# Giving one of three interleaved lanes an earlier rank in a four-layer graph network kernel

## The chip, the cores and the metric

The kernel runs on one core of one Trainium2 chip. The metric is the device time of one execution in microseconds (us); where several executions are given, it is their median.

## What is computed

The input is `x` (16 x 1024 x 128) and a sparse symmetric-pattern `adj` (16 x 1024 x 1024): about 1.6% of the places off the diagonal, and all on it, are not zero. Four graph layers follow, each applied to a normalized, rectified copy of `x` and added to it:

```python
h = relu(layernorm(x)); x = x + L0(h, adj)   # relu(W [h, (h^T adj)^T / degree] + b)
h = relu(layernorm(x)); x = x + L1(h, adj)   # leaky(W (adj/degree) h + b)
h = relu(layernorm(x)); x = x + L2(h, adj)   # two rounds, below
h = relu(layernorm(x)); x = x + L3(h, adj)   # softmax attention over the neighbours, then elu
```

Layer 2 is the costly one. In each of two rounds it scores every edge (n, m) with a small network, weighs the adjacency with it, sends messages and updates the nodes:

```python
scores = sigmoid(relu(a[:, :, None] + b[:, None] + be1) @ We2 + be2)
messages = (adjacency * scores) @ x
x = layernorm(x + (relu([x, messages] @ Wu1 + bu1) @ Wu2 + bu2)) * gamma + beta
```

## The kernel before, in words

Only the edges are scored. The 1024 x 1024 places of a batch are 64 blocks of 128 x 128; a block (t, u) above the diagonal and its mirror make one "bucket" of up to 320 edges (480 on the diagonal). There are 36 buckets, in nine groups of four (`GROUPS`, L371 to L377). For each bucket the kernel builds one-hot tiles, `on` and `om` and their transposes `onT` and `omT`, with which TensorE gathers node features to edges and scatters scores back to blocks. These tiles live in a pool with as many buffers as one batch needs and four more off the diagonal, so those of the next batch take their places as they come free.

The work of a batch is split into three generators, called lanes here:

- `first` (L533): layer 0 on eight rows of blocks (loads at L547 and L551, degree at L552, transposes at L557, products at L239), layer 1 (`layer1`, L261, rows at L268 to L273), the norm of layer 2, and `build` (L637), which makes the one-hot tiles group by group: a product for ranks (L648, L652), then for each bucket `far` (L618), `on` (L622), `onT` (L660), `omT` (L667) and `om` (L674), with products at L631 and L663 between them.
- `main` (L904): the rounds' lane. Round one, a node update (`update`, L277 to L313), round two. A round (`round`, L690) first splits products of the nodes with the weights into two halves (`split`, L682), and then for each of nine groups gathers (L783, L787, and `hid` at L799), scores (L811, row at L824, turned at L836 to L842), scatters (L855, L876), applies the sigmoid and the adjacency (L884, L885) and sends messages (L890). Scatters and messages lag the gathers by a group and more. Its adjacency loads are issued at L761 on SyncE's queue. At a round's end the messages are copied out (L913).
- `last` (L924): the node update after round two, and layer 3 with eight rows (L336 to L358).

Each lane has its own scratch buffers in SBUF and its own bank or banks of PSUM (L398: two for the rounds, one for `first`, one for `last`); the rounds have four more banks for scores, scatters and messages.

Three lanes are in flight together: `main` of batch b, `last` of batch b - 1 and `first` of batch b + 1. `run` (L943) sets up this for each batch, and `weave` (L965) takes steps from the lanes in turn: each generator yields an estimate of what it emitted, and the lane with the smallest share of its total (`MAIN_US`, `LAST_US`, `FIRST_US`) goes next. `main` is always lane 0. The first batch's `first` and the last batch's `last` stand alone.

The order of emission is not quite the order in the program. Each instruction gets a rank from a counter as it is emitted. When the program is put together, each engine takes, by estimated times, the instruction of the lowest rank among those whose inputs and buffers are ready. The order thus found on each engine is fixed in the program; semaphores then make the engines wait for one another on the chip. Where two lanes compete for an engine, the rank decides; where only one is ready, its rank does not matter.

The norm chain that all lanes have is `center` (L193 to L204): a sum (L196), a scaling (L197), a subtraction (L198), a square (L200), a sum (L201), a scaling (L202), all on VectorE, and a power on POOL (L203). In the node update it stands between L305 and L308 to L311.

Of the kernel before, what the change touches and what calls it, by code (L numbers as in the profile page):

```python
# [1 line left out]

# [38 lines left out]
MAIN_US = 248.0  # L41
FIRST_US = 112.0
LAST_US = 95.0


SPLIT = (0, 1, 0, 0, 1, 0, 1, 0)
# [3 lines left out]
def tile_four_gnn_layers(  # L50
# [335 lines left out]
    class Edges:  # L386
# [556 lines left out]
        def run(self):  # L943
# [8 lines left out]
            for b in range(B):  # L952
                s = self.next
                lanes = [(self.main(s, b), MAIN_US)]
                if b:
                    lanes.append((self.last(done, b - 1), LAST_US))
                if b + 1 < B:
# [7 lines left out]
        def weave(self, lanes):  # L965

            out_of = [[0.0, i, gen, us] for i, (gen, us) in enumerate(lanes)]
            while out_of:
                least = min(out_of, key=lambda v: v[:2])
                us = next(least[2], None)  # L970
                if us is None:
                    out_of.remove(least)
                else:
                    least[0] += us / least[3]
# [155 lines left out]
```

## Time and profile before

| what | us |
|---|---|
| median of 3 executions | 6016.66 |
| lowest and highest | 6015.26, 6018.78 |
| the profiled execution, its own time | 6019.67 |
| its span in the profile | 6017.8 |
| TensorE busy (PE) | 5596.7 |
| TensorE weight loads (PEld), beside the products | 4114.2 |
| VectorE busy (DVE) | 4223.4 |
| ScalarE busy (ACT) | 3237.2 |
| one batch in the steady part, from round two to round two | about 361 |

The mean granted clock of TensorE is 0.978 of full speed. Busy times are sums over the span of one execution; TensorE's products are pipelined and their ends are modelled, so that a full TensorE is not one at its peak. A group's line gives the code line, the engine, what is written and read, the count, the busy time and the mean of one in ns. A product of fp32 operands shows as two records. In a table of stretches the busy times are of the given window alone.

### The profile page before, as it was taken

Reading aid. Unit: us, or ns where it says so; the run is one execution under the profiler, and the core shown is the slowest. Engines: PE = TensorE matmul, PEld = TensorE weight load, DVE = VectorE, ACT = ScalarE, POOL = GpSimd, SP = SyncE. Lnnn points to the kernel's source line nnn. Section 1 sums busy time; section 2 is a strip of 40 time slices with the busy share of each in tenths; the row PEclk is TensorE's granted clock in tenths of the full one; section 3 lists DMA queues with packets and bytes.
Section 4 is the critical chain, followed back from the end, with each engine's and each line's share of the span. In section 5 each row is a group of like instructions: output and inputs, shape, how many; then the busy total and the mean of one; then the engine's idle time right before and its main releaser. Section 6 shows DMA issues by size and latency. Waiting matters only on the chain.

```text
span 6017.8 us, 117792 instructions
## 1 busy us (share of the span) xinstructions
PE 5596.7 (93%) x49152; PEld 4114.2 (68%) x49152; DVE 4223.4 (70%) x7718; ACT 3237.2 (54%) x5945; POOL 170.1 (3%) x105
## 2 busy tenths in 40 slices
PE   4899999999999999999999999999999999999984
PEld 4667767676776777767676676776767677676664
DVE  4566777767677686777767677686777767677665
ACT  2545474645647455474645647455474645647442
POOL 0000000000000000000000000000000000000000
PEclk8999999999999999999999999999999999999987
DMA  5322314233242422414233242422414233242110
GB/s 149 99 82 81 120 54 122 90 106 99 64 131 67 120 88 85 123 54 122 90 102 103 60 134 68 120 88 85 123 54 122 90 101 103 60 132 63 45 61 30
DMA packets 694189, 554.81 MB, mean 92 GB/s; under 512 B 29200, under 2 KB 630160, under 8 KB 693648
## 3 DMA queue, kind: packets, MB, share of 16 engines
q1 hardware_dynamic: 688384, 545.37, 30.4%
q8 instruction: 387, 6.34, 0.4%
q10 hardware_dynamic: 5264, 1.84, 0.1%
q14 instruction: 154, 1.26, 0.1%
HBM read 446.44 MB, written 100.66 MB: 91 GB/s over the span
## 4 chain that ended last, share of the span: by engine, by line
PE 70%; DVE 12%; ACT 9%; DMA 6%; issue 2%; POOL 2%; SPq 0%; ACTq 0%; DVEq 0%; POOLq 0%
PE p L876 9%; PE sc L811 9%; PE nb L239 8%; PE pre L783 7%; PE pre L787 7%; PE msg L890 6%; PE h L286 4%; DMA at<-in_adj_dram 2%; PE pn L631 2%; PE pq L663 2%; PE tn L557 2%; PE pm L631 2%; POOL st L203 1%; PE xn L298 1%; ACT hid L799 1%
## 5 line engine op out<-in xcount | busy, mean ns | idle before, releaser
L799 ACT ACTIVATE hid<-pre,be_sb 128x320 f32<-128x320 f32 (+1 forms) x2048 | 1094.6, 544 | 1029.9 <-PE pre L787 1017.8
L811 PE MATMUL sc<-hid,slide_s 128*32 128x320 f32 (+1 forms) x4096 | 665.3, 461 | 3.6 <-DVE u L842 2.1
L855 DVE TENSOR_TENSOR val<-onT,u 128x384 f32<-128x384 fp8e4 (+1 forms) x1152 | 612.0, 581 | 5.2
L667 DVE TENSOR_TENSOR omT<-pq,odd 128x384 fp8e4<-128x384 f32 (+1 forms) x576 | 336.6, 585 | 388.1 <-PE pq L663 381.2
L876 PE MATMUL p<-val,omT 128*128 128x128 f16 x7424 | 589.6, 219 | 12.5 <-ACT upd L884 10.7
L890 PE MATMUL msg<-upd,xf 128*128 128x128 f32 (+3 forms) x2944 | 595.4, 326 | 4.0 <-DVE upd L885 3.9
L783 PE MATMUL pre<-on,part_a 128*128 128x320 fp8e4 (+1 forms) x2304 | 561.4, 315 | 20.3 <-ACT hid L799 11.5
L787 PE MATMUL pre<-om,part_b 128*128 128x320 fp8e4 (+1 forms) x2304 | 558.9, 314 | 0.0
L876 PEld LDWEIGHTS <-omT 128*128 128x128 fp8e4 x7424 | 484.3, 96 | 87.1 <-issue 30.9
L885 DVE TENSOR_TENSOR upd<-upd,adj 128x512 f32<-128x512 f32 x512 | 350.5, 687 | 132.0 <-ACT upd L884 129.2
L855 DVE TENSOR_TENSOR val<-omT,u 128x384 f32<-128x384 fp8e4 x896 | 442.1, 551 | 0.0
L783 PE MATMUL pre<-on,part_b 128*128 128x320 fp8e4 x1792 | 421.2, 299 | 0.1
L876 PE MATMUL p<-val,onT 128*128 128x128 f16 x5376 | 416.9, 219 | 4.4 <-ACT upd L884 4.4
L890 PEld LDWEIGHTS msg<-upd,xf 128*128 128x128 f32 x2944 | 395.4, 191 | 32.5 <-issue 12.3
L787 PE MATMUL pre<-om,part_a 128*128 128x320 fp8e4 x1792 | 399.8, 299 | 0.0
L876 PEld LDWEIGHTS <-onT 128*128 128x128 fp8e4 x5376 | 352.3, 96 | 43.2 <-issue 16.7
L884 ACT ACTIVATE upd<-p 128x512 f32<-128x512 f32 x512 | 305.2, 596 | 136.6 <-PE p L876 120.9
L783 PEld LDWEIGHTS <-part_a 128*128 128x128 f16 x2304 | 192.7, 98 | 265.7 <-issue 249.9
L618 ACT ACTIVATE far<-iota,mid 128x384 f16<-128x384 f16 (+1 forms) x576 | 354.5, 639 | 34.6 <-DVE on L622 25.1
L660 ACT ACTIVATE onT<-pn 128x384 fp8e4<-128x384 f32 (+1 forms) x576 | 295.6, 514 | 93.8 <-PE pn L631 92.1
L674 ACT ACTIVATE om<-pm 128x320 fp8e4<-128x320 f32 (+1 forms) x576 | 266.0, 462 | 141.9 <-PE pm L631 139.2
L787 PEld LDWEIGHTS <-part_b 128*128 128x128 f16 x2304 | 220.7, 98 | 138.4 <-issue 39.6
(200 smaller groups left out, 9946.8 us busy)
## 6 DMA issues: line engine op xcount, KB each, us to landing
at<-in_adj_dram SPq DMA_DIRECT2D x128, 512.0 KB, 4.0
ct<-in_adj_dram SPq DMA_DIRECT2D x128, 512.0 KB, 4.4
a<-in_adj_dram SPq DMA_DIRECT2D x128, 512.0 KB, 3.6
adjT<-tn SPq DMA_DIRECT2D x128, 512.0 KB, 5.0
l<-adjT SPq DMA_DIRECT2D x128, 512.0 KB, 4.6
adj<-adjT SPq DMA_DIRECT2D x256, 256.0 KB, 3.5
adj<-adjT SPq DMA_DIRECT2D x384, 64.0 KB, 2.9
adj<-adjT SPq DMA_DIRECT2D x128, 192.0 KB, 3.2
```

The costliest lines, as they stand in the source:

```text
L239: nc.tensor.matmul(ps, mat[:, k], z[:, k], start=(k == 0), stop=(k == T - 1))
L618: nc.scalar.activation(far[:, : ck * P], self.iota2[:, : ck * P], AF.Abs, bias=s.mid[:, i : i + 1])
L667: nc.vector.tensor_tensor(omT.rearrange("p (k m) -> p k m", m=P), pq[:, :ck], self.odd[:, :ck, None].to_broadcast([P, ck, P]), op=OP.is_eq ...
L783: nc.tensor.matmul(pre[:, :c], ra[0][:, k, ra[1]], on[:, :c], start=(k == 0), stop=False)
L787: nc.tensor.matmul(pre[:, :c], rb[0][:, k, rb[1]], om, start=False, stop=(k == 1))
L799: nc.scalar.activation(hid[:, :c], pre[:, :c], AF.Relu, bias=be1_sb[:, self.l : self.l + 1])
L811: nc.tensor.matmul(self.sc[g * G : (g + 1) * G, : self.c], self.path.slide[:, self.l, G - 1 - r : 2 * G - 1 - r], self.hid[self.done + g][ ...
L855: nc.vector.tensor_tensor(pair[:, i % 2, :ck], right[:, :ck], u[:, :, j % J, j // J : j // J + 1].to_broadcast([P, ck, P]), op=OP.mult,)
L876: nc.tensor.matmul(self.ps[d][:, i], left[:, k], halves[:, k, :, h], start=(k == 0 and h == 0), stop=(k == self.ck - 1 and h == 1),)
L884: nc.scalar.activation(upd, self.ps[d], AF.Sigmoid, scale=1.0 / S_SCALE)
L885: nc.vector.tensor_mul(upd, upd, self.adj[:, d * Q : (d + 1) * Q])
L890: nc.tensor.matmul(self.msg[:, lo * P : hi * P], self.xf[:, mb], up, start=False, stop=True, skip_group_check=True,)
```

## The change

In `weave`, the steps of lane 0, the rounds' lane, are emitted inside a context that lowers the rank counter by 600; on leaving it the counter gets back the value that it had before. So each step of the rounds' lane is ranked as if it had been emitted 600 places earlier, and since its instructions no longer move the counter on, the places are those of the other two lanes' instructions. The steps that the lanes take, their order of emission, the tiles, the buffers and the arithmetic stay as they are.

```diff
-from contextlib import ExitStack
+from contextlib import ExitStack, nullcontext
...
+AHEAD = 600
...
             while out_of:
                 least = min(out_of, key=lambda v: v[:2])
-                us = next(least[2], None)
+
+                with tc.high_priority(offset=AHEAD) if least[1] == 0 else nullcontext():
+                    us = next(least[2], None)
                 if us is None:
                     out_of.remove(least)
                 else:
```

## The prediction

> **What bounds the kernel now.** I read the page's busy line first, then the busy time by stretches through one steady batch, then VectorE's order in the one stretch where TensorE is not full.
>
> ```profile
> span 6017.8 us, 117792 instructions
> PE 5596.7 (93%) x49152; PEld 4114.2 (68%) x49152; DVE 4223.4 (70%) x7718; ACT 3237.2 (54%) x5945; POOL 170.1 (3%) x105
> ```
>
> TensorE is busy for 93% of the span, and no other engine comes near. The missing 421 us are what an order can win. The table by stretches shows where they lie (columns: from:to, length, then the busy us of PE, PEld, DVE, ACT, POOL).
>
> ```profile
> 2182.00:2328.00 146.00, 142.49 (x1377) 100.02 (x1375) 112.00 (x220) 109.17 (x209) 3.63 (x2) 1.00 0.20 61
> 2328.00:2339.00 11.00, 10.83 (x76) 7.09 (x75) 5.11 (x8) 6.42 (x13) 0.00 (x0) 1.00 0.24 67
> 2339.00:2501.00 162.00, 158.86 (x1400) 118.66 (x1399) 114.92 (x212) 76.67 (x135) 5.28 (x3) 1.00 0.41 118
> 2501.00:2543.00 42.00, 34.58 (x224) 28.50 (x223) 29.86 (x42) 9.84 (x18) 1.64 (x1) 0.92 0.43 137
> ...
> 5880.00:6018.00 138.00, 63.83 (x292) 52.56 (x290) 74.89 (x91) 28.14 (x44) 3.27 (x2) 0.69 0.10 31
> 0.00:180.00 180.00, 91.40 (x612) 81.64 (x613) 80.89 (x173) 51.52 (x92) 8.51 (x13) 0.78 0.47 133
> ```
>
> The first four lines are one period of 361 us: second round (2182 to 2328), the next batch's first split, first round (to 2501), and the node update between the rounds (to 2543). TensorE idles 3.5, 0.2, 3.1 and 7.4 us in them, 14.2 in all. So half of a batch's idle time lies in 42 us in which the rounds' lane has no round to run. The start (88.6 us idle) and the tail (74.2 us idle) are the work of one lane alone. The timeline of VectorE shows what the update waits for:
>
> ```profile
> 2158.09 1.22 DVE L305 TENSOR_TENSOR y<-y,xf 128x1024 f32<-128x1024 f32 x1
> 2159.23 1.21 DVE L348 TENSOR_REDUCE nmax<-e 128x1 f32<-128x1024 f32 x1
> 2160.36 1.21 DVE L196 TENSOR_REDUCE st_y<-y 128x8 f32<-128x1024 f32 x1
> 2161.48 0.34 DVE L270 SCALAR_TENSOR_TENSOR o<-nb,deg,b_bc 128x128 f32<-128x128 f32 x1
> 2161.74 0.16 DVE L197 TENSOR_SCALAR st_y<-st_y 128x8 f32<-128x8 f32 x1
> 2161.81 0.16 DVE L356 RECIPROCAL rsum<-rsum 128x1 f32<-128x1 f32 x1
> 2161.94 1.23 DVE L198 TENSOR_TENSOR y<-y,st_y 128x1024 f32<-128x1024 f32 x1
> ```
>
> Each step of the update's norm (L305, L196, L197, L198) is followed by one of another lane (L348, L270, L356). From the first L303 at 2152.18 to the end of L311 at 2173.12 the chain takes 20.9 us, of which its own twelve VectorE steps and one on POOL are 13.1.
>
> **What the Trainium skill says.** "TensorE: Matmul & The Clock Gate", section "Architectural detail", says that ACT and VectorE work strictly first in, first out, and only weight loads pass other work on TensorE; so an order fixed in the program is the order on the chip. The timeline agrees: the update waits 1.2 us for another lane's L348. "Perfetto Trace Analysis", section "Optimization Strategy", says that stretches with different busiest engines may gain by being interleaved. Here the update stretch has VectorE at 29.9 of 42 us and TensorE at 34.6. The same page, "Identifying the Most-Contended Engine", warns that matmul busy time is no measure of distance to the peak; weight loads at 68% agree, so I use busy time only to find holes. The same page, "Matmuls", wants independent groups to rotate through PSUM banks; the lane that builds the one-hot tiles has one bank, which matters below.
>
> **The change part by part.** No instruction is added or removed. The rounds' lane (`main`) gets ranks 600 lower; the counter is put back afterwards, so places are counted in the other lanes' instructions. From the loops I count about 1,050 of `first` and 370 of `last` per batch, 1,420 in all: 600 places are some 0.4 of a batch.
>
> Part one, what stands beside the update. Now it stands beside layer 3's rows and layer 1's end (L348, L270 above). Ahead by 0.4 of a batch, it stands beside the next batch's layer 0 rows (L552 to L254). From the groups by line, a layer 3 row has 6.4 us of VectorE (L339 0.28, L341 1.28, L344 0.69, L345, L346 and L348 3.65, L356 0.16, L357 0.35) for 3.6 us of TensorE (transposes 179/128 = 1.4, products 282/128 = 2.2). A layer 0 row has 2.6 us of VectorE (L552 1.22, L553 0.15, L564 108/128 = 0.85, L254 0.35) for 3.4 of TensorE (166/128 = 1.3 and 270/128 = 2.1). In the chain's 20.9 us VectorE has 7.8 us left over: layer 3 rows yield 7.8/6.4 x 3.6 = 4.4 us of TensorE work, layer 0 rows by that count 10.3. But alone in the machine at the start such a row took 9.5 us (first and last L552 at 27.5 and 94.0, seven rows), so 20.9 us hold 2.2 rows, 7.5 us of TensorE. The gain is 7.5 - 4.4 = 3.1 us a batch. It lies on the path that sets the end, since the next round can't start before the update.
>
> Part two, the update's own chain. At best the strangers between its steps go, 20.9 - 13.1 = 7.8 us of chain; at worst nothing, since a step isn't ready at the moment the one before it ends and something else slips in. The strict alternation above speaks for the second. I take 0.
>
> Part three, the build of the one-hot tiles (L648 to L674). Now it runs beside round two (first to last L674: 2198 to 2351) and is done before the next round one is far in. Ahead by 0.4 of a batch, round one takes each tile soon after it is built. That cover is what is spent: its cost is between 0 and the rival below. I take 0, because the last five groups take (2351-2277)/5 = 15 us each and round one needs 17.2 a group (L824 from 2345.5 to 2483.2 in eight steps).
>
> Part four, what moves along. SyncE: the lane's 56 adjacency loads a batch (L761) and its saves and reloads of xT move past the other lanes' loads. L761 already holds SyncE up for 1,010 us in all behind L885, 15.6 at the longest; a row load behind it can be late by that, or come earlier by as much when L885 is done earlier. Two row buffers cover it; I take 0. POOL: two of six power steps a batch move past the others', 1.6 to 1.8 us each, with POOL 3% busy; 0. ScalarE: 182 table loads in the rounds and rows, 1.28 us each (91 at L884, 76 at L349, 15 at L361), depend on how sigmoid and exp alternate; a batch could have some five more or fewer, 6 us either way, on an engine 54% busy; 0.
>
> Part five, both ends. The last batch's main comes before all of the last lane beside it (370 places are fewer than 600). Its rows now end near 5807, 73 us before the rounds do, and those 73 us hide the delay; without cover it would cost up to eight rows of 9.9 us (L348 from 5929.9 to 5999.3 in seven steps). I take 0 at both ends.
>
> Sum: 15 x 3.1 = 47 us less. Against the profiled execution's 6019.67 (span 6017.8 and 1.9 around it) that is 5973; this execution is 3 us over the median of 6016.66, so the median goes to 5970.
>
> **The rivals.** (A) The forecast, 5970. (B) The update's hole closes and the scattered holes shrink too: 9 of the 14.2 us a batch go, 15 x 9 = 135 us, 5880. For it: the alternation would vanish if the program's order prefers the rounds. Against: the alternation itself.
>
> (C) The hole only moves: another lane's chain stands beside it and TensorE's fixed work stays. 6015. For it: every lane has a norm chain (L196 to L218) of the same kind.
>
> (D) Slower: the build becomes what round one waits for. One mechanism: each bucket's three products share the lane's single bank, and each is behind the rounds' instructions in rank. The first four groups now take (2276.9 - 2194.6)/4 = 20.6 us each. At that pace nine groups cost 9 x (20.6 - 17.2) = 31 us more in round one, and the round waits 20.6 us for its first group. With TensorE idle as in today's stretch without rounds, 7.6 of 42 us or 0.19, that is 9.8 us; less the 3.1 of part one, 6.7 a batch, 100 us in all: 6115. It decides from 9 x (pace - 17.2) x 0.19 = 3.1 on, a pace of 19 us a group. For it: ScalarE and VectorE already wait 381 us (L667), 139 us (L674) and 92 us (L660) for the build's products. Against: the later groups' 15 us in a full TensorE.
>
> **How the numbers follow.** A 0.38, B 0.13, C 0.13, D 0.36. A's own range is 5930 to 6004. The whole range is 5875 to 6120: it leaves out less than half of B and of D, some 0.2. About 0.2%, 12 us, is what a measurement of this kernel can tell from no change. A and B make faster 0.50; C with the near edges of A and D makes same 0.13; slower is 0.37.
>
> **What would show it.** Right: in the stretch between rounds TensorE idles about 4.5 instead of 7.5 us, layer 0 rows (L552, L557) stand in it, and a batch takes some 358 us. Part two wrong: the update's steps follow each other without strangers, and the chain is near 13 us. Part three wrong, thus D: L783 or its weight loads wait for L622 or L674, and the steps between L824 in round one rise over 19 us. C: the period stays at 361 us with the idle time elsewhere. Part five wrong: L348 of batch 14 runs on after the last round, and the tail exceeds 138 us.

## The result, and the profile after

The changed kernel takes 7411.88 us (median of four; 7406.9 to 7412.45) against 6015.96 in the same runs: 1.2319 times as long, 95% interval 1.2297 to 1.234. The forecast was 5970. Every batch is longer: the period goes from 361.2 to 448.0 us. First the busy line of the page:

```profile
span 7410.1 us, 118186 instructions
PE 6518.3 (88%) x49152; PEld 4282.8 (58%) x49152; DVE 4297.3 (58%) x7718; ACT 3272.2 (44%) x5963; POOL 162.2 (2%) x105
```

The same 49,152 records keep TensorE busy for 922 us more, and it idles for 471 us more (7410.1 - 6518.3 = 891.8 against 421.1). So there are two losses. The prediction had taken it that a program which only reorders its work leaves TensorE's busy time alone.

Where the busy time grew is in the groups by line. The score products (L811 before, L813 after):

```profile
L811 PE MATMUL sc<-hid,slide_s 128*32 128x320 f32 (+1 forms) x4096 | 665.3, 461 | 3.6 <-DVE u L842 2.1 <-DVE srow L823 1.5
```

```profile
L813 PE MATMUL sc<-hid,slide_s 128*32 128x320 f32 (+1 forms) x4096 | 1289.0, 467 | 6.2 <-ACT hid L801 3.0 <-DVE u L844 0.6
```

The mean of one is the same, 461 and 467 ns, but the time in which at least one runs has nearly doubled. Counted from each record's start to the next one's on TensorE (no longer than its own end), these products take 1177 us instead of 611: 566 of the 922. They overlap less. TensorE's timeline shows why. Before:

```profile
2379.86 0.62 PE L876 MATMUL p<-val,omT 128*128 128x128 f16 x8
2380.41 0.74 PE L811 MATMUL sc<-hid,slide_s 128*32 128x320 f32 x8
2381.09 0.45 PE L783 MATMUL pre<-on,part_a 128*128 128x320 fp8e4 x2
```

After:

```profile
2907.65 0.43 PE L785 MATMUL pre<-on,part_a 128*128 128x320 fp8e4 x2
2908.01 0.72 PE L813 MATMUL sc<-hid,slide_s 128*32 128x320 f32 x2
2908.67 0.23 PE L654 MATMUL pr<-tri,has 128*128 128x128 f16 x1
2908.74 0.22 PE L650 MATMUL pr<-cnt,low 128*128 128x128 f16 x1
2908.79 0.43 PE L785 MATMUL pre<-on,part_b 128*128 128x320 fp8e4 x2
2909.16 0.73 PE L813 MATMUL sc<-hid,slide_s 128*32 128x320 f32 x2
```

A row of scores is four products (L811 in `dots`), each into its own 32 partitions (a strip); with fp32 operands each is two records. Four together (x8) take 0.74 us, and one alone (x2) 0.72. Over the whole trace of before, by the count from start to start, the median per record is 330 ns in a run of two, 166 in a run of four, 112 in six and 90 in eight. Before, 319 products stood alone; after, 1430 of 2048 do.

The idle time is in the stretches (columns as before; the last three are the mean granted clock of TensorE, the busy share of the DMA engines and GB/s). The first line is round one of a batch; the other two are the node update and round two, whose first row of scores comes at 3118.7:

```profile
2840.00:3067.00 227.00, 196.40 (x1478) 120.99 (x1477) 125.42 (x213) 106.05 (x194) 3.27 (x2) 0.96 0.11 32
3067.00:3103.00 36.00, 29.80 (x171) 22.86 (x169) 21.88 (x33) 9.89 (x16) 1.64 (x1) 0.91 0.52 152
3103.00:3277.00 174.00, 168.69 (x1360) 116.86 (x1359) 112.80 (x228) 83.04 (x154) 5.10 (x3) 1.00 0.40 119
```

Round one takes 227 us with 30.6 idle, where it took 162 with 3.1. The clock adds to the busy time: over the whole span TensorE is busy for 380 us at half the full clock, where it was 177 before. There an L878 record that another follows takes 107 ns in the median, at full clock 58. So some 100 of the 922 us, half of the 203 us more, are the clock (an estimate from these figures). What is left of the 922 us after scores and clock is spread over the other products and was not taken apart.

The view of `om`'s line, which ends the build of a bucket, names the wait (first the idle time before it on ScalarE, then who waited for it):

```profile
  PE pm L633: 727.7, 384
...
  PE pre L789: 96.5, 178
```

Before, that idle time was 139.2 us (170 times), and no product of the rounds waited for `om`. TensorE also waits inside the build, for `omT`, where it did so for 10.6 us before:

```profile
PE pm L633 <- DVE omT L669: 160.9, 230, 1.8
```

These two waits make up 247 of the 471 us more. Now round one's first row of scores follows the batch's first `om` by 25 us, before by 147 (means of batches 4 to 12).

### The profile page after: what moved, and what is told of

The parts are those of the page before. It is cut to its first block, busy times and chain, and to the rows that moved or that the text cites. A ratio compares the mean times of both kernels' runs of the same rounds, so it can differ in the third digit from the quotient of the medians.

```text
span 7410.1 us, 118186 instructions
## 1 busy us (share of the span) xinstructions
PE 6518.3 (88%) x49152; PEld 4282.8 (58%) x49152; DVE 4297.3 (58%) x7718; ACT 3272.2 (44%) x5963; POOL 162.2 (2%) x105
## 4 chain that ended last, share of the span: by engine, by line
PE 68%; DVE 14%; ACT 9%; DMA 3%; issue 3%; POOL 2%; ACTq 0%; SPq 0%; POOLq 0%; DVEq 0%
PE sc L813 15%; PE nb L241 9%; PE pre L785 8%; PE p L878 8%; PE pre L789 7%; PE msg L892 5%; PE h L288 3%; DVE val L857 2%; ACT hid L801 2%; DMA ct<-in_adj_dram 2%; PE xn L300 2%; PE pq L665 2%; DVE omT L669 1%; ACT om L676 1%; PE pm L633 1%
## 5 line engine op out<-in xcount | busy, mean ns | idle before, releaser
L801 ACT ACTIVATE hid<-pre,be_sb 128x320 f32<-128x320 f32 (+1 forms) x2048 | 1060.1, 541 | 1192.0 <-PE pre L789 1089.5
L813 PE MATMUL sc<-hid,slide_s 128*32 128x320 f32 (+1 forms) x4096 | 1289.0, 467 | 6.2 <-ACT hid L801 3.0
L878 PE MATMUL p<-val,omT 128*128 128x128 f16 x7424 | 700.0, 221 | 16.7 <-DVE val L857 14.4
L892 PE MATMUL msg<-upd,xf 128*128 128x128 f32 (+3 forms) x2944 | 628.3, 330 | 20.7 <-DVE upd L887 20.4
L878 PEld LDWEIGHTS <-omT 128*128 128x128 fp8e4 x7424 | 525.2, 98 | 196.6 <-issue 137.0
L826 DVE TENSOR_SCALAR srow<-sc,be_s 128x320 f32<-128x320 f32 (+1 forms) x288 | 169.2, 587 | 786.2 <-PE sc L813 786.1
L878 PE MATMUL p<-val,onT 128*128 128x128 f16 x5376 | 555.2, 220 | 20.5 <-ACT upd L886 19.6
L886 ACT ACTIVATE upd<-p 128x512 f32<-128x512 f32 x512 | 304.5, 595 | 543.6 <-PE p L878 526.5
L887 DVE TENSOR_TENSOR upd<-upd,adj 128x512 f32<-128x512 f32 x512 | 351.4, 687 | 279.2 <-ACT upd L886 277.2
L813 PEld LDWEIGHTS sc<-hid,slide_s 128*32 128x32 f32 x4096 | 236.1, 108 | 364.4 <-issue 247.2
L878 PEld LDWEIGHTS <-onT 128*128 128x128 fp8e4 x5376 | 387.8, 97 | 89.9 <-issue 75.2
L241 PE MATMUL nb<-z,ct 128*128 128x128 f32 x2048 | 330.4, 310 | 79.4 <-DMA ct<-in_adj_dram 62.2
```

What stands on the lines that cost most here:

```text
L241: nc.tensor.matmul(ps, mat[:, k], z[:, k], start=(k == 0), stop=(k == T - 1))
L801: nc.scalar.activation(hid[:, :c], pre[:, :c], AF.Relu, bias=be1_sb[:, self.l : self.l + 1])
L813: nc.tensor.matmul(self.sc[g * G : (g + 1) * G, : self.c], self.path.slide[:, self.l, G - 1 - r : 2 * G - 1 - r], self.hid[self.done + g][ ...
L878: nc.tensor.matmul(self.ps[d][:, i], left[:, k], halves[:, k, :, h], start=(k == 0 and h == 0), stop=(k == self.ck - 1 and h == 1),)
L886: nc.scalar.activation(upd, self.ps[d], AF.Sigmoid, scale=1.0 / S_SCALE)
L887: nc.vector.tensor_mul(upd, upd, self.adj[:, d * Q : (d + 1) * Q])
```

## The theories

Theory 1: TensorE no longer has a queue of ready rounds' products. With the earlier rank, a score product is taken as soon as its own input is there, and other work comes between it and its three companions. Theory 2: round one's instructions now outrank the build, the build slows, and round one waits for it. Each run below is timed beside the kernel before (6009.9 to 6013.3 us).

## The experiments

**The four scores together, in both kernels.** Each of the first three products waits for the last of the four inputs too, recorded by `behind` as a dependence, and the four get the earliest rank of all (an offset of 3000).

```diff
-                    nc.scalar.activation(
+                    self.at = nc.scalar.activation(
...
+                    self.made.append(self.at)
...
-                    for g in range(J):
-                        nc.tensor.matmul(
+                    with tc.high_priority(offset=3000):
+                        for g in range(J):
+                            mm = nc.tensor.matmul(
...
+                            if g < J - 1:
+                                behind(mm, self.made[self.done + J - 1])
```

> The changed kernel, but the four score products of a row (L811 before) wait for the last of their four inputs and then rank first of all, so that they stand together on TensorE. Theory 1 (the earlier rank lets each score product go alone as soon as its own input is ready, and a lone one costs as much as four together): the products' 1177 us fall to some 370, and the time falls from 7412 to between 6500 and 6850. Theory 2 (round one waits for the build of the one-hot tiles, and TensorE's longer busy time only fills that wait): the time stays above 7100.

> The kernel before with the same edit: the four score products of a row together. Theory 1: 319 lone products of before join their rows, their 611 us fall to some 370 and TensorE is full, so about 5780 (5740 to 5860). Theory 2 has nothing to say on packing: 5950 to 6020, since the rounds' order is what counts.

Measured: 6564.73 us in the changed kernel (1.0921 of before; interval 1.09 to 1.0943) and 5846.09 in the kernel before (0.9728; interval 0.9711 to 0.9744). Both as theory 1 has it. All 512 rows now stand together, at 85 ns a record in the median:

```profile
L822 PE MATMUL sc<-hid,slide_s 128*32 128x320 f32 (+1 forms) x4096 | 407.9, 471 | 12.6 <-ACT hid L808 6.9 <-DVE u L855 0.6
```

```profile
L820 PE MATMUL sc<-hid,slide_s 128*32 128x320 f32 (+1 forms) x4096 | 399.5, 462 | 15.0 <-DVE u L853 1.8 <-DVE srow L834 1.0 <-ACT hid L806 0.9
```

The edit takes 847 us off the changed kernel and 166 off the one before. The difference, 681 us, is what the change cost by parting the scores; it comes from a subtraction, and the edit also gives the scores the earliest rank, which was not tried by itself. What is left between the two packed kernels, 6564.73 - 5846.09 = 719 us, is not the scores, which take 374 and 365 us of TensorE. In the changed one TensorE still idles 47 us a batch (17.6 in the other), and round one is the place:

```profile
2513.00:2719.00 206.00, 173.35 (x1516) 123.85 (x1515) 130.44 (x219) 108.82 (x200) 3.27 (x2) 0.96 0.14 43
2719.00:2767.00 48.00, 39.73 (x251) 29.62 (x250) 32.83 (x50) 18.42 (x30) 1.64 (x1) 0.96 0.56 178
2767.00:2909.00 142.00, 135.77 (x1311) 106.34 (x1308) 102.59 (x213) 78.21 (x145) 5.21 (x3) 1.00 0.40 121
```

So 32.7 us are idle in 206, and 6 to 8 in each of the other two stretches. Idle time is not all: TensorE is also busy for 5621.4 us instead of 5372.5, with 363 us instead of 163 of it at half clock.

**Lone scores in the kernel before.** No lane is put ahead; `dots` issues what it has.

```diff
                     self.hid.append(hid)
+                    if i:
+                        self.dots()
...
-                while len(self.hid) - self.done >= J:
-                    r = self.done // J
-                    for g in range(J):
+                while len(self.hid) > self.done:
+                    r, g = self.done // J, self.done % J
...
-                    self.done += J
+                    self.done += 1
```

> The kernel before, ranks untouched, but each score product is emitted as soon as its own input is, with other products between, so that 1567 instead of 319 stand alone. Theory 1: at 330 ns a record for a lone product some 570 us more, 6450 to 6650. Theory 2: no build is waited for, so 6000 to 6100.

Measured: 6751.64 us (1.1232; interval 1.121 to 1.1255). Theory 1's direction, and 100 us over its range: by the count from start to start the scores take 1267 us of TensorE where they took 611, 656 more of the 740.

```profile
L813 PE MATMUL sc<-hid,slide_s 128*32 128x320 f32 (+1 forms) x4096 | 1386.1, 461 | 53.5 <-ACT hid L799 12.0 <-DVE u L844 2.3 <-DVE srow L825 1.5
```

Idle time stays at 15.2 us a batch. Loss of company alone thus costs as much as half of the change did.

**Half the lead.** `AHEAD` is 300, without and with the scores together.

> The changed kernel with 300 places instead of 600, so that the build keeps a lead over round one. Theory 1 (1265 lone products): some 400 us above before, 6350 to 6500, and TensorE's idle time about as before. Theory 2: near before, 6000 to 6150. Both at work in the changed kernel: as theory 1, with the wait for the build gone.

> Four score products together, and the rounds' lane 300 places ahead. Theory 2 for what is left of the loss once the products stand together (at 600 places round one follows the build at 25 us and waits for it; at 300 it follows at some 100 us and doesn't): between 5830 and 5920, TensorE idle some 15 us a batch. If instead any earlier rank of the rounds costs time, by whatever it does to the other lanes: about half way between the two packed runs at 0 and 600 places, 6150 to 6250.

Measured: 6593.02 us without (1.0969; interval 1.0947 to 1.099). 1265 products stand alone, TensorE idles 12.6 us a batch, no more than before, and round one follows the build at 102 us. This separates the losses: at 300 places the waits for the build are gone (3.7 us for `om` and 10.7 for `omT`), and TensorE is busy for 568 us more, 457 of them in the scores (theory 1, whose range was 93 us too low). With the scores together it is 6055.27 (1.0075; interval 1.0058 to 1.0091), between the two expectations: better than half way, but 209 us over the packed kernel at no lead. Idle time is 22.6 us a batch against 17.6, and TensorE is busy 5486 us against 5372.5 (312 against 163 of it at half clock), so some loss that is neither the scores nor the wait for the build is there already.

**The build ahead too.** In the packed changed kernel, each step of `build` also gets 600 places.

```diff
-            yield from self.build(s, has, name)
+            yield from ahead(self.build(s, has, name), AHEAD)
```

> Four score products together, the rounds' lane 600 places ahead as in the change, and the steps that build the one-hot tiles 600 places ahead too. Theory 2, with the rank as the reason that the build is slow: the build gets its lead back, 5850 to 6100. If the build is slow of itself once round one stands beside it (its one PSUM bank, its own waits): no change, 6450 to 6650.

Measured: 6849.38 us (1.1397; interval 1.1374 to 1.142), slower than either case had it. Yet the build takes 133 us instead of 210, and round one's steps 15.3 us a group instead of 23.4, at a distance of only 17 us. So the build is not slow of itself; its rank made it so. The wait has moved instead: the batch's first `om` now comes 120 us after the last score row of the batch before, since layers 0 and 1, which the build follows in its lane, keep the later rank. In the batch shown the rows of round two stand from 2798 to 2886, the first `om` comes at 3004 and the messages are copied out at 3072; that stretch holds the idle time:

```profile
2610.00:2744.00 134.00, 127.06 (x1293) 91.86 (x1292) 77.85 (x156) 80.41 (x160) 0.00 (x0) 1.00 0.16 48
...
2798.00:3072.00 274.00, 218.40 (x1956) 164.21 (x1956) 186.06 (x345) 132.52 (x245) 7.47 (x4) 0.94 0.30 91
```

**Round one at its old rank.** Packed, 600 places ahead except in round one.

```diff
+                self.one = l == 0
                 yield from self.round(s, l, s.xf, xT, name)
+                self.one = False
...
-with tc.high_priority(offset=AHEAD) if least[1] == 0 else nullcontext():
+with tc.high_priority(offset=AHEAD) if least[1] == 0 and not self.one else nullcontext():
```

> Four score products together; the rounds' lane 600 places ahead as in the change, except in round one, which keeps the rank of before. Theory 2 (at 600 places the build stands after round one in rank, and round one waits for it): round one comes after the build again, TensorE idles 15 to 20 us a batch, 5830 to 5960. If it is the lead of the lane as such that costs time, whatever the order of build and round one: 6200 to 6550, since update and round two still go ahead.

Measured: 6055.55 us (1.0072; interval 1.0052 to 1.0092). 509 of the 719 us are gone, and round one is whole again:

```profile
2318.00:2490.00 172.00, 163.47 (x1541) 120.86 (x1538) 120.30 (x216) 97.73 (x186) 3.65 (x2) 1.00 0.30 89
2490.00:2559.00 69.00, 57.00 (x380) 45.55 (x379) 48.72 (x79) 24.43 (x43) 5.13 (x2) 0.88 0.46 141
```

It idles 8.5 us instead of 32.7, and the build takes 151 us, though round one follows it at only 29 us. So it is round one's rank that cost most, not its being side by side with the build. The edit puts round one back behind all the work of the other lanes, and not behind the build alone; but of TensorE's two waits for the build, 97.6 us for `om` and 154.0 for `omT` in the packed changed kernel, none and 18.4 are left. The result is still 96 us over the range of theory 2. The update now takes 69 us with 12 idle; why these 209 us remain, as at 300 places, isn't settled.

**The hole between the rounds.** Packed, ranks of before; only the node update and the splits go 300 places ahead.

> Four score products together, ranks of before, and only the node update between the rounds and the splits after it 300 places ahead. If the hole of TensorE between the rounds (7.5 us a batch) comes from the update's rank on VectorE: 5740 to 5800. If other lanes' steps slip in between whatever the rank: 5825 to 5865, as with the products together alone.

Measured: 5888.9 us (0.9796; interval 0.978 to 0.9813), 43 us slower than packing alone and above both expectations. The update's chain on VectorE takes 19.8 us instead of 20.8 in the packed kernel: a better rank keeps almost no stranger out.

**Four scores in one strip.** Packed, ranks of before; the second row of a group off the diagonal writes its four products to the first 32 partitions, with the flags of the accumulation set to match. The scores of the other three strips are left without that row.

```diff
-self.sc[g * G : (g + 1) * G, : self.c],
+self.sc[g * G : (g + 1) * G, : self.c] if r == 0 else self.sc[:G, : self.c],
```

> Ranks of before, four score products together; but in the second row of the groups off the diagonal all four write the first strip of 32 partitions, so the scores of the other three strips are left without that row. If the four cost as little as one because they run at once in four strips of the array: 224 x 8 records go from 85 to 330 ns, 440 us more than with four strips, 6230 to 6320. If it is enough that they follow one another: no change, 5830 to 5870.

Measured: 6244.99 us (1.0391; interval 1.037 to 1.0412), 399 over the four-strip run. The four products of all 512 rows still stand together, but by the count from start to start they take 729 us instead of 365.

```profile
L820 PE MATMUL sc<-hid,slide_s 128*32 128x320 f32 (+1 forms) x4096 | 762.2, 459 | 19.8 <-DVE srow L834 1.0 <-DVE u L853 0.6 <-ACT hid L806 0.6
```

So adjacency is not what makes four cost as little as one; four strips at once are. One strip is here also one place of output, and the run doesn't tell the two apart.

**Other leads.** All packed: 100 places for the rounds; 300 for the build alone; and, with the turn reversed, 150 for the other two lanes.

> Four score products together, the rounds' lane 100 places ahead. If the loss grows evenly with the places (209 us at 300): 5890 to 5940. If it sets in only when round one reaches the build: 5830 to 5865. If a small lead fills TensorE's hole between the rounds: below 5820.

> Four score products together, ranks of before for the rounds, and only the build of the one-hot tiles 300 places ahead. The build has a lead of 140 us over round one already, so theory 2 expects no gain from more: 5830 to 5880. If the build still costs TensorE holes by its waits: below 5810.

> Four score products together, and the turn of the change reversed: the other two lanes 150 places (of the rounds' instructions) ahead, the rounds' lane at its rank. If the slope from 600 over 300 and 100 places to 0 goes on past 0: below 5835. If the order of before is near the best for these lanes: 5840 to 5900.

Measured: 5883.28 us (0.9786; interval 0.977 to 0.9803), 5910.67 (0.9831; interval 0.9814 to 0.9847) and 6216.77 (1.0344; interval 1.0326 to 1.0361). The first lies between its first two cases, the second 30 us above its range, and the third 371 us above no lead, far over both of its cases. Packed, the time over the rounds' lead is 5846 at 0, 5883 at 100, 6055 at 300 and 6565 at 600 places: it rises by 0.4, then 0.9, then 1.7 us a place, and the order of before is the best of those tried. With the scores together it beats both kernels: 5846.09 us.

## Why the prediction was wrong

The forecast had the wrong sign, and the time lies far above the range's end of 6120.

- "No instruction is added or removed", and so a fixed busy time, was the step that failed first. It holds for the count, not for the time: order decides whether four products run at once. The page carried the sign: the group's 4096 records of 461 ns are 1,888 us and its busy time was 665, an overlap of 2.8 that the sum never asked about. It went to 1.5. Price 681 us, from the two packed kernels; the case was in none of the rivals, and C takes "TensorE's fixed work" for granted.
- Part three took the build's cost at 0 because its late groups took 15 us in a full TensorE. That pace was measured when the build stood level in rank with round two. Behind round one in rank the build took 239 us in all, from 153, and round one 27.2 us a group, 23.4 with the scores together, where it had needed 17.2. Rival D named this mechanism and its sign (gathers that wait for the build's tiles, steps over 19 us), but took 20.6 us as its pace and 0.19 as TensorE's idle share, hence 100 us. Round one's rank cost 509. Two slips in D's working matter less: 7.6 of 42 us is 0.18, and the table has 7.4; and the threshold of 19 us a group leaves out the wait for the first group, which even at 17.2 us a group is 17.2 x 0.19 = 3.3 us, more than the 3.1 it is weighed against.
- Part one expected layer 0 rows to fill the update's stretch and 3.1 us a batch to come of it. From the copy of the messages to the first score product of round two TensorE's idle time went from 8.7 to 7.3 us (means of batches 4 to 12), 1.5 a batch: the sign right, the size half, and little beside 28 us more idle time in round one. Layer 0 rows do stand there (L554 at 3088.0 and 3096.9 in the batch shown), but layer 3 as well (L350 at 3068.8).
- Part two took 0 of 7.8 us for the update's own chain. It went from 21.0 to 19.0 (same means), and between the packed kernels, with the update alone ahead, from 20.8 to 19.8. Nearly right.
- Part four: the table loads rose from 182 to 200 (L363 has fewer, L886 and L351 more), 18 x 1.28 = 23 us on an engine 44% busy. Not the cause. SyncE's wait for L887 at the adjacency loads rose from 1,010 to 2254.6 us, but no wait for these loads shows at L887 in the trace. Loads behind them may come later: TensorE's wait for `ct` at layer 0 (L241) went from 20.6 to 62.2 us, little of 1,400; no run here took it alone.
- Part five: the tail after the last copy of messages is 138.3 us, from 137.6. Right.

So 681 us for the scores and 509 for round one's rank are accounted for, what the lower clock adds included; the other 209 come with the earlier rank of the lane, and their cause is open.

The Trainium skill has the mechanism in "TensorE: Matmul & The Clock Gate", section "Part 3: Packing small matmuls": products at different strips of the array run concurrently, and matmuls themselves are never reordered. The runs agree: four strips at 0.68 us (8 x 85 ns) against 0.66 for one, and nothing pulls a lone product back to its row. The prediction drew on that page for the queues and passed over the form 128*32 in the group's line.

## What to carry to other kernels

Before changing an order, compare each group's count times mean with its busy time. The two records of a lone product here give 1.4 (2 x 461 ns in 0.66 us); the group's 2.8 said that its products lived from standing together. An order which takes each as soon as it is ready destroys that; tie such instructions together explicitly.

A lane that is put ahead can slow the very lane that feeds it: at their meeting point the consumer should not outrank its feeder (509 us here). Putting the feeder ahead too was no remedy; it moved the wait (6849.38 us). And a distance left between the two does not make the lead free: packed, at 300 places, round one followed the build at 95 us, and 209 us were lost.

## What was not expected of the hardware

One product of 128 x 32 weights on 320 columns of fp32 holds TensorE for 0.66 us, four in different strips for 0.68, and four in one strip for about 2.5 (an estimate: the 224 such rows added 399 us, 1.8 us each). A single record of another kind between two products is enough to lose the overlap: in the changed kernel one scatter record (L878) stands so 93 times. The product before it and the one after take 0.66 us each in the median, and the scatter record takes 160 ns, where the median of all such records is 58.
